# A selective-scan network on one core: one broadcast of B for two scans, and the skip term as a diagonal product

## The chip, the cores and the metric

The kernel runs on one core of one Trainium2 chip. The metric is the device time of one execution in microseconds (us). The core has a tensor engine (PE in the profile, with its weight loads as PEld), a vector engine (DVE), a scalar engine (ACT), GpSimd (POOL) and a sync engine (SP), which issues the transfers here. PE writes its products to PSUM[...]; the other tiles lie in SBUF.

## The reference

An input of 32 images (512 channels, 32x32 pixels) goes through four blocks in turn, with a group normalisation over 16 channels between them: channel weights from a discrete cosine transform (L0), a grouped 3x3 convolution (L1), a pyramid of selective scans (L2), and a channel attention that samples neighbouring channels (L3). The change lies in L2. Cut to what matters:

```python
def _ssm(x, xw, dtw, dtb, Al, Dv, g, be):       # x: [B, D=256, L], n = 16 states
    xd = einsum('bdl,kd->blk', x, xw)
    dts, Bs, Cs = split(xd)                      # 8, 16 and 16 columns
    delta = softplus(einsum('blr,dr->bld', dts, dtw) + dtb)
    dA  = exp(delta[..., None] * -exp(Al))       # per channel and state
    dBx = delta[..., None] * Bs[:, :, None, :] * xt[..., None]
    h = h * dA + dBx                             # a scan over L
    y = sum over n of h * C  +  xt * Dv          # Dv: the skip term
    return layernorm(y, g, be)
```

Each image has three resolutions: 1024 pixels (twice, forward and backward), 256 and 64 pixels (both directions). The scan is run for 256 channels and 16 states.

## The kernel before

**Tiles and units.** A scan tile has 128 partitions, which are 32 channels times 4 states, and 1024 columns. At full resolution (function `fine`) one direction of one image takes 2 halves `d` of the channels x 4 groups `k` of states x 4 groups `q` of channels = 32 such units; 64 calls of `fine` make 2048 units. The coarse resolutions (function `both`) pack several pieces in one tile and make 640 more scans, of which each pair shares one product tile.

One fine unit is this:

- PE multiplies `sb` (B, held in bfloat16 parts) with `sel_b[:, k, :]`, in two matmuls of 512 columns, into a PSUM tile `pb` (L1266). This puts the four states' rows of B onto the 128 partitions. It depends on `k` but not on `q`. The ring `pb` has two tiles of two banks each.
- ACT computes `da` = exp(delta * A) from the loaded tile `dt` (L1273); the ring `da` has two tiles.
- DVE multiplies `pb` in place with delta * x, which lies in the same `dt` (L1279).
- DVE scans over the 1024 columns with `da` and `pb` into `h` (L1212, the helper `scan`); six `h` tiles.
- POOL multiplies `h` with the loaded broadcast of C, `cb` (L1287).

After four units (`q` = 0 to 3) PE sums over the states by a product with `sel_y`, into two PSUM accumulators of one bank each, `y0` and `y1b`, one for each half of the columns (L1295). After the four `k` of one `d`, the scan input is loaded to `yv` (L1304), and DVE adds the skip term for each half in one instruction, yv = yv * Dv + accumulator (L1309). That frees the accumulators for the next `d`. A layer norm follows after both `d` (`layer_norm`, L1142 to L1165).

`both` treats its own skip term otherwise: the helper `skip_weights` (L1214) lets ACT write a diagonal matrix of Dv to the tile `dg`, a ring of one; PE adds its product with the input to the accumulator (L1476), and ACT copies the accumulator to SBUF (L1488).

**Order.** Nothing is issued in source order. Every operation is recorded with an engine, an estimated duration, what it reads and writes, and a key: a due time of 100 per image, with 84 scan units to an image. `Clock.key(ahead)` gives the key of the current unit less so many units. At the end `Plan.order` walks through a model of the engines: whenever an engine is free it takes the ready operation with the lowest key, if the ring buffers that it needs are free. Rings marked as ordered (`pb` is one) hand out their buffers in order of the buffers' keys, which is the key of the first operation that asks unless one is set. The outcome is a fixed order on each engine, and the engines then run in that order, waiting on each other. The constants on top (`B_AHEAD` for the broadcast, `A_AHEAD` for the exponential, `L_AHEAD` for loads, `DB_AHEAD` for the product) say how many units ahead of its scan an operation is due. `INPUTS` holds the keys, within 100 per image, between which the first convolution's products for `f1` are spread (function `scan_inputs`). Several images are in work at once: while one is scanned, the next ones' transforms, convolutions and projections fill PE, ACT and POOL.

Of the kernel before, what the change touches and what calls it, by code (L numbers as in the profile page):

```python
# [11 lines left out]
ALU = mybir.AluOpType  # L12
# [3 lines left out]
HW = 1024  # L16
IMG = 32
GC = 16
NS = 16
NQ = 4  # L20
# [4 lines left out]
HB = 512  # L25
# [3 lines left out]
UNITS = 84  # L29

FRONT = (30.9, 63.6)
INPUTS = (109.0, 112.0)
Z = (86.2, 90.1)
DOWN = 114.3
LOWER = (11.8, 36.0)
# [4 lines left out]
SPECTRA = (51.7, 128.4)  # L40
EVACUATE = 85.0
LN_LATE = 10.1
B_AHEAD, A_AHEAD, L_AHEAD, DB_AHEAD = 5.8, 5.9, 14.7, 1.3


class Buf:
# [175 lines left out]
def t_mm(n, count=1):  # L222
    return count * (0.06 + 1.02 * n / 512)


def t_dve(n):
    return 0.11 + n / 970
# [11 lines left out]
def kernel(ctx: ExitStack, tc: tile.TileContext, t: dict, out: bass.AP):  # L239
    nc = tc.nc  # L240
# [108 lines left out]
    xw, A, Dv, G, BE, dtb = [], [], [], [], [], []  # L349
# [46 lines left out]
    pl = Plan(rings)  # L396
# [16 lines left out]
    def pe(fn, dur, r, w, key, acq=()):  # L413
        return pl.op("PE", dur, fn, r, w, key, acq)

    def act(fn, n, r, w, key, ptr=False, acq=()):
        return pl.op("ACT", t_act(n, ptr), fn, r, w, key, acq)

    def dve(fn, n, r, w, key, acq=()):
        return pl.op("DVE", t_dve(n), fn, r, w, key, acq)  # L420
# [793 lines left out]
    def skip_weights(lv, d, key):  # L1214

        dg = pl.buf("dg")
        act(
            lambda: nc.scalar.activation(dg.t, ident, AF.Copy, scale=Dv[lv][:, d : d + 1]), P, [ready],
            [dg], key, True,
        )  # L1220
        return dg
# [10 lines left out]
    def fine(lv, f, pre, S, rev, ck):  # L1232


        sb, cd, dd = pre.pop(f"{lv}_{HW}")
        pl.cross = pl.BESIDE
        if rev:
            raised(S["y1"], S["y2"], ck.key())
        pl.cross = pl.CROSS
        yv = []  # L1240
        for d in range(2):
            acc = [pl.buf("y0"), pl.buf("y1b")]
            dt = []
            for q in range(4):
                ch = slice((d * 4 + q) * 32, (d * 4 + q + 1) * 32)
                z = pl.buf("dt")
                dt.append(z)
                spread(
                    lambda z=z: z.t, lambda i, ch=ch: dd.t[:, ch, :].rearrange("a c l -> c a l"),
                    P * HW * 8, [(dd, (d, h)) for h in range(2)], [z], ck.key(L_AHEAD - q),  # L1250
                )
            for k in range(NS // NQ):
                cb = pl.buf("cb")
                spread(
                    lambda cb=cb: cb.t,
                    lambda i, k=k: cd.t[k * NQ + i : k * NQ + i + 1].to_broadcast([32, HW]),
                    P * HW * 4, [cd], [cb], ck.key(5),
                )
                hs = []
                for q in range(4):  # L1260
                    g = d * 4 + q
                    pb, da, h = pl.buf("pb"), pl.buf("da"), pl.buf("h")

                    def bcast(pb=pb, k=k):
                        for cols in halves:
                            nc.tensor.matmul(  # L1266
                                pb.t[:, cols], lhsT=sel_b[:, k, :], rhs=sb.t[:, cols],
                                start=True, stop=True,
                            )

                    pe(bcast, 0.55, [sb], [pb], ck.key(B_AHEAD))
                    act(
                        lambda da=da, z=dt[q], k=k, g=g: nc.scalar.activation(  # L1273
                            da.t, z.t[:, 1, :], AF.Exp, scale=A[lv][:, k, g : g + 1]
                        ),
                        HW, [dt[q]], [da], ck.key(A_AHEAD), True,
                    )
                    dve(
                        lambda pb=pb, z=dt[q]: nc.vector.tensor_mul(pb.t, z.t[:, 0, :], pb.t), HW,  # L1279
                        [dt[q], pb], [pb], ck.key(DB_AHEAD),  # L1280
                    )
                    pl.op(
                        "DVE", 2.21, lambda h=h, da=da, pb=pb: scan(h.t, da.t, pb.t, rev), [da, pb], [h],
                        ck.key(),
                    )
                    pool(
                        lambda h=h, cb=cb: nc.gpsimd.tensor_mul(h.t, h.t, cb.t), HW, [h, cb], [h],  # L1287
                        ck.key(),
                    )
                    hs.append(h)  # L1290
                    ck.u += 1
                for i, cols in enumerate(halves):
                    def add(i=i, cols=cols, hs=hs, acc=acc, k=k):
                        for q in range(4):
                            nc.tensor.matmul(  # L1295
                                acc[i].t[q * 32 : (q + 1) * 32, :], lhsT=sel_y, rhs=hs[q].t[:, cols],
                                start=(k == 0), stop=(k == NS // NQ - 1),
                            )

                    pe(add, 1.3, hs, [acc[i]], ck.key(2))  # L1300
            y = pl.buf("yv")
            yv.append(y)
            dma(
                lambda y=y, d=d: nc.sync.dma_start(y.t, f.t[d]), P * HW * 4, [(f, d)],  # L1304
                [(y, 0), (y, 1)], ck.key(8),
            )
            for i, cols in enumerate(halves):
                dve(
                    lambda i=i, cols=cols, acc=acc, y=y, d=d: nc.vector.scalar_tensor_tensor(  # L1309
                        y.t[:, cols], in0=y.t[:, cols], scalar=Dv[lv][:, d : d + 1], in1=acc[i].t,  # L1310
                        op0=ALU.mult, op1=ALU.add,
                    ),
                    HB, [(y, i), acc[i]], [(y, i)], ck.key(3),
                )
        pl.cross = pl.BESIDE
        if not rev:
            S["y1"] = pl.buf("y1")
        y1 = S["y1"]
        for i, cols in enumerate(halves):
            yb = [(yv[d], i) for d in range(2)]  # L1320

            def yc(d, cols=cols):
                return yv[d].t[:, cols]

            def yo(d, cols=cols):
                return y1.t[:, d, cols]

            ob = [(y1, (d, i)) for d in range(2)]
            layer_norm(
                lv, yc, yb, yc if rev else yo, yb if rev else ob, HB, ck.key() + (0.0 if rev else LN_LATE)  # L1330
            )
            if not rev:
                continue
            g = pl.buf("g2")
            for d in range(2):
                dma(
                    lambda d=d, g=g, cols=cols: nc.sync.dma_start(g.t[:, d, :], S["zs"].t[d, :, cols]),
                    P * 2048, [(S["zs"], (d, i)), yb[d]], [(g, d)], ck.key(),
                )
                pool(  # L1340
                    lambda d=d, yo=yo, yc=yc: nc.gpsimd.tensor_add(yo(d), yo(d), yc(d)), HB,
                    [yb[d], ob[d]], [ob[d]], ck.key(),
                )
                pool(
                    lambda d=d, yo=yo, g=g: nc.gpsimd.tensor_mul(yo(d), yo(d), g.t[:, d, :]), HB,
                    [ob[d], (g, d)], [ob[d]], ck.key(),
                )

    def both(lv, f, pre, ysum, below, n, ck):


        sb, cd, dd = pre.pop(f"{lv}_{n}")
# [12 lines left out]
        acc = [pl.buf("y0"), pl.buf("y1b")]  # L1365
# [8 lines left out]
        for d in range(2):  # L1374
            dt = pl.buf("dt")
# [9 lines left out]
                )  # L1385
            for k0 in range(0, 4, nk):
                pb = pl.buf("pb")

                def bcast(pb=pb, k0=k0):
                    for h in range(2):  # L1390
                        if nk == 1:
                            src = sb.t.rearrange("p (o l) -> p o l", o=1).to_broadcast([96, 2, n])
                            nc.tensor.matmul(  # L1393
                                pb.t[:, halves[h]].rearrange("p (o l) -> p o l", o=2),
                                lhsT=sel_b[:, k0, :], rhs=src, start=True, stop=True,
                            )
                            continue
                        for k in range(h * nk // 2, (h + 1) * nk // 2):
                            src = sb.t.rearrange("p (o l) -> p o l", o=1).to_broadcast([96, 4, n])
                            nc.tensor.matmul(  # L1400
                                pieces(pb.t)[:, k, :, :], lhsT=sel_b[:, k0 + k, :], rhs=src,
                                start=True, stop=True,
                            )
# [21 lines left out]
                for r in range(2):  # L1425
                    da, h = pl.buf("da"), pl.buf("h")
# [46 lines left out]
            dg = skip_weights(lv, d, ck.key(8))  # L1473
# [7 lines left out]
        y = pl.buf("yv" if n > 64 else "yc")  # L1481
# [398 lines left out]
```

## Time and profile before

| | |
|---|---|
| median of three timed runs | 11386.0 us (11367.82 to 11386.98) |
| profiled execution, its own time | 11408.22 us |
| its span | 11406.1 us |
| granted PE clock, mean | 0.861 |
| busy: DVE / POOL / PE / ACT | 9938.1 / 9544.0 / 9375.9 / 8259.6 us |
| fine scans and coarse scans together (L1212) | 2688, 2275 ns each |
| broadcasts of B at full resolution (L1266) | 2048, of two matmuls each |
| skip-term instructions at full resolution (L1309) | 256 |

The durations in the sections below come from the one profiled execution. A row of a group gives line, engine, operation, output and inputs with shapes, count, then busy us in all and mean ns of one, then the idle time of the engine just before such instructions, and what ended most of it. A row of the waits reads: who waited, for whom, us in total, how often, the longest in us.

### The profile page before, as it was taken

To read this page: it belongs to the slowest core of one execution; us is meant where nothing else is said; L and a number is where in the kernel's file an instruction comes from. 1 tells how busy PE (TensorE), PEld (TensorE's weight loads), DVE (VectorE), ACT (ScalarE), POOL (GpSimd) and SP (SyncE) were. 2 spreads that over 40 slices of the span, in tenths; PEclk is the share of its full clock that TensorE was granted. 3 is DMA by queue.
4 is the path that set the end of the run, shared out by engine and by line. 5 is a ranking of instruction groups with operands and counts; after the bars stand their busy time and mean duration, and the time that the engine had idled before them with its cause. 6 is when DMAs were issued, how large, how long until landed. Compare 5 with 4: busy or idle time off the path is not lost. (4 is left out here: it accounts for less than half of the span.)

```text
span 11406.1 us, 152013 instructions
## 1 busy us (share of the span) xinstructions
PE 9375.9 (82%) x47512; PEld 4155.3 (36%) x47512; DVE 9938.1 (87%) x8861; ACT 8259.6 (72%) x15684; POOL 9544.0 (84%) x7759
## 2 busy tenths in 40 slices
PE   7888888888888888888888888888888888878765
PEld 4444433334333343333333343333433333332221
DVE  1875889998899989999899999899889998999997
ACT  4677777777778777777777777777777776667664
POOL 2775878898889888888888988898888898889885
PEclk7888889888889888898888988898898987888877
DMA  5665677776767777777767777777677766776654
GB/s 153 167 173 164 182 197 195 186 194 186 212 179 202 188 188 191 204 198 202 191 183 189 204 199 189 189 189 186 190 199 196 187 180 181 199 192 185 168 134 136
DMA packets 931019, 2116.80 MB, mean 186 GB/s; under 512 B 240033, under 2 KB 372537, under 8 KB 917785
## 3 DMA queue, kind: packets, MB, share of 16 engines
q1 hardware_dynamic: 930192, 2107.01, 69.5%
q8 instruction: 376, 6.16, 0.2%
q14 instruction: 433, 3.55, 0.1%
q10 hardware_dynamic: 18, 0.09, 0.0%
HBM read 1677.04 MB, written 429.52 MB: 185 GB/s over the span
## 5 line engine op out<-in xcount | busy, mean ns | idle before, releaser
L1212 DVE TENSOR_TENSOR_SCAN h_all<-da,pb 128x1024 f32<-128x1024 f32 x2688 | 6069.7, 2275 | 296.2 <-ACT da L1435 78.3
L1287 POOL TENSOR_TENSOR h_all<-h_all,cb 128x1024 f32<-128x1024 f32 x2048 | 4818.1, 2363 | 859.9 <-DVE h_all L1212 582.7
L1273 ACT ACTIVATE da<-dt,w_Al 128x1024 f32<-128x1024 f32 x2048 | 2337.1, 1145 | 1171.5 <-DVE h_all L1212 902.5
L1279 DVE TENSOR_TENSOR pb<-dt,pb 128x1024 f32<-128x1024 f32 x2048 | 2462.4, 1218 | 322.7 <-PE pb L1266 276.1
L1266 PE MATMUL pb<-sb,sel_b 96*128 96x512 bf16 x4096 | 1390.4, 426 | 888.0 <-DVE h_all L1212 797.2
L1455 POOL TENSOR_TENSOR h_all<-h_all,cb 128x1024 f32<-128x1024 f32 x640 | 1509.3, 2363 | 20.8 <-DVE h_all L1212 7.4
L1266 PEld LDWEIGHTS <-sel_b 96*128 96x128 bf16 x4096 | 402.4, 107 | 2032.8 <-issue 1998.0
L952 PE MATMUL mm<-x,wt 128*128 128x512 f32 x2048 | 1027.8, 626 | 54.8 <-ACT x L482 18.9
L899 PE MATMUL mm<-pk,wk 99*32 99x512 f32 (+1 forms) x6024 | 904.2, 688 | 113.8 <-DMA pk<-in_xp 19.9
L1444 ACT ACTIVATE da<-dt,w_Al 128x255 f32<-128x255 f32 x2048 | 899.4, 500 | 97.6 <-DVE h_all L1212 79.7
L1295 PE MATMUL y<-h_all,w_sel_y 128*32 128x512 f32 x4096 | 784.4, 724 | 33.5 <-POOL h_all L1287 27.2
L617 PE MATMUL mm<-w_dct,sx 128*128 128x128 f32 x3968 | 651.2, 319 | 94.6 <-ACT sg L460 24.7
L617 PEld LDWEIGHTS mm<-w_dct,sx 128*128 128x128 f32 x3968 | 583.6, 225 | 237.7 <-ACT sg L460 50.1
L1295 PE MATMUL y1b<-h_all,w_sel_y 128*32 128x512 f32 x4096 | 647.7, 663 | 0.0
L952 PE MATMUL mm<-y,w_out_w 128*128 128x512 f32 x1024 | 576.2, 655 | 0.1
L952 PEld LDWEIGHTS mm<-x,wt 128*128 128x128 f32 x2048 | 387.5, 198 | 492.5 <-issue 284.5
L1112 POOL TENSOR_TENSOR g<-g,g 128x512 f32<-128x512 f32 (+2 forms) x384 | 392.9, 1023 | 144.6 <-ACT g L1111 134.5
L1096 PE MATMUL mm<-xd,dtw 64*128 64x512 f32 (+2 forms) x768 | 417.4, 628 | 79.2 <-ACT xd L1066 11.7
L1142 PE MATMUL mm<-ln,ones_d 128*128 128x512 f32 (+1 forms) x768 | 433.1, 662 | 59.9 <-ACT ln L1154 30.7
L1407 DVE TENSOR_TENSOR pb<-dt,pb 128x1024 f32<-128x1024 f32 x320 | 387.7, 1218 | 108.5 <-PE pb L1393 86.6
L974 PE MATMUL mm<-f,wt 128*128 128x256 f32 (+1 forms) x1984 | 421.6, 357 | 21.7 <-ACT f L982 6.0
L1142 PE MATMUL mm<-yv,ones_d 128*128 128x512 f32 x640 | 380.6, 691 | 40.1 <-ACT mm L921 7.2
(292 smaller groups left out, 16188.4 us busy)
## 6 DMA issues: line engine op xcount, KB each, us to landing
dt<-dd SPq DMA_DIRECT2D x2048, 256.0 KB, 7.3
cb<-cd SPq DMA_DIRECT2D x2048, 128.0 KB, 4.8
pk<-in_xp SPq DMA_DIRECT2D x753, 297.0 KB, 5.5
dd<-g SPq DMA_DIRECT2D x256, 512.0 KB, 5.1
xr<-x SPq DMA_DIRECT2D x128, 512.0 KB, 6.3
yv<-fs SPq DMA_DIRECT2D x128, 512.0 KB, 5.1
dt<-ddm SPq DMA_DIRECT2D x512, 128.0 KB, 3.9
sx<-in_x SPq DMA_DIRECT2D x124, 512.0 KB, 4.7
```

The source lines that it names most:

```text
L617: nc.tensor.matmul(ps.t[:, j * P : (j + 1) * P], lhsT=sx.t[:, 1, i : i + P], rhs=dct, start=True, stop=True,)
L899: nc.tensor.matmul(ps.t[32 * q : 32 * q + 32, r0 * IMG : r1 * IMG].rearrange("p (r k) -> p r k", k=IMG), lhsT=wk.t[:, q, 32 * dy : 32 * dy ...
L952: nc.tensor.matmul(ps.t, lhsT=w(k)[:, m * P : (m + 1) * P], rhs=r()[:, cols], start=(k == 0 and not opened), stop=(k == len(rhs) - 1),)
L1142: lambda d=d: nc.tensor.matmul(ps.t[:, 0:n], lhsT=ones_d, rhs=of(d), start=(d == 0), stop=(d == 1)),
L1212: nc.vector.tensor_tensor_scan(v[0], v[1], v[2], 0.0, ALU.mult, ALU.add)
L1266: nc.tensor.matmul(pb.t[:, cols], lhsT=sel_b[:, k, :], rhs=sb.t[:, cols], start=True, stop=True,)
L1273: lambda da=da, z=dt[q], k=k, g=g: nc.scalar.activation(da.t, z.t[:, 1, :], AF.Exp, scale=A[lv][:, k, g : g + 1]),
L1279: lambda pb=pb, z=dt[q]: nc.vector.tensor_mul(pb.t, z.t[:, 0, :], pb.t), HW,
L1287: lambda h=h, cb=cb: nc.gpsimd.tensor_mul(h.t, h.t, cb.t), HW, [h, cb], [h],
L1295: nc.tensor.matmul(acc[i].t[q * 32 : (q + 1) * 32, :], lhsT=sel_y, rhs=hs[q].t[:, cols], start=(k == 0), stop=(k == NS // NQ - 1),)
L1444: lambda da=da, quads=quads, q=q, g=g, body=body, k0=k0: nc.scalar.activation(pieces(da.t)[:, 0, q, body], quads(1)[:, q, body], AF.Exp, s ...
L1455: lambda h=h, k0=k0: nc.gpsimd.tensor_mul(pieces(h.t), pieces(h.t), cbv()[:, k0 : k0 + nk, :].rearrange("p k (o l) -> p k o l", o=1).to_br ...
```

## The change

Three things are changed. At full resolution the broadcast of B is made once for two units that follow each other (`q` = 0, 1 and `q` = 2, 3): the first unit's product goes from the broadcast's tile `src` to a second `pb` tile, the second unit's product is made in place in `src`. The keys by which the two tiles are handed out are set by hand, and so is that of the coarse scans' tile. Second, the skip term at full resolution is made as `both` makes it: a diagonal matrix from ACT, a float32 product on PE that closes the accumulation, and a copy of the accumulator to `yv` on ACT, in place of the instruction on DVE. Third, three key constants move.

```diff
-INPUTS = (109.0, 112.0)
+INPUTS = (109.0, 123.2)
...
-B_AHEAD, A_AHEAD, L_AHEAD, DB_AHEAD = 5.8, 5.9, 14.7, 1.3
+B_AHEAD, A_AHEAD, L_AHEAD, DB_AHEAD = 8.0, 5.9, 14.7, 1.8
...
-                    pb, da, h = pl.buf("pb"), pl.buf("da"), pl.buf("h")
-
-                    def bcast(pb=pb, k=k):
+                    da, h = pl.buf("da"), pl.buf("h")
+
+
+                    if q % 2 == 0:
+                        src, pb = pl.buf("pb"), pl.buf("pb")
+                        src.key, pb.key = (ck.key(2.9), len(pl.ops)), (ck.key(1.0), len(pl.ops))
+                    else:
+                        pb = src
+
+                    def bcast(pb=src, k=k):
...
-                    pe(bcast, 0.55, [sb], [pb], ck.key(B_AHEAD))
+                    if q % 2 == 0:
+                        pe(bcast, 0.55, [sb], [src], ck.key(B_AHEAD))
...
                     dve(
-                        lambda pb=pb, z=dt[q]: nc.vector.tensor_mul(pb.t, z.t[:, 0, :], pb.t), HW,
-                        [dt[q], pb], [pb], ck.key(DB_AHEAD),
+                        lambda pb=pb, src=src, z=dt[q]: nc.vector.tensor_mul(pb.t, z.t[:, 0, :], src.t), HW,
+                        [dt[q], src], [pb], ck.key(DB_AHEAD),
                     )
...
-                                start=(k == 0), stop=(k == NS // NQ - 1),
+                                start=(k == 0), stop=False,
...
+            dg = skip_weights(lv, d, ck.key(8))
             for i, cols in enumerate(halves):
-                dve(
-                    lambda i=i, cols=cols, acc=acc, y=y, d=d: nc.vector.scalar_tensor_tensor(
-                        y.t[:, cols], in0=y.t[:, cols], scalar=Dv[lv][:, d : d + 1], in1=acc[i].t,
-                        op0=ALU.mult, op1=ALU.add,
+                pe(
+                    lambda i=i, cols=cols, acc=acc, y=y, dg=dg: nc.tensor.matmul(
+                        acc[i].t, lhsT=dg.t, rhs=y.t[:, cols], start=False, stop=True
                     ),
-                    HB, [(y, i), acc[i]], [(y, i)], ck.key(3),
+                    t_mm(HB), [(y, i), dg], [acc[i]], ck.key(3),
+                )
+                act(
+                    lambda i=i, cols=cols, acc=acc, y=y: nc.scalar.copy(y.t[:, cols], acc[i].t), HB,
+                    [acc[i]], [(y, i)], ck.key(3),
                 )
...
             for k0 in range(0, 4, nk):
                 pb = pl.buf("pb")
+                pb.key = (ck.key(2.9), len(pl.ops))
```

## The prediction

> **What bounds the kernel now.** I read the page first, then the busy time by stage, the DVE groups with shapes kept apart, the waits, and the instruction order of both programs, which is fixed when they are built. First the page: the span and part 1.
>
> ```profile
> span 11406.1 us, 152013 instructions
> PE 9375.9 (82%) x47512; PEld 4155.3 (36%) x47512; DVE 9938.1 (87%) x8861; ACT 8259.6 (72%) x15684; POOL 9544.0 (84%) x7759
> ```
>
> No engine is full: DVE leads, 1468 us idle, with POOL 394 us of work behind it. By stage (busy us of PE, PEld, DVE, ACT, POOL, then granted clock):
>
> ```profile
> 0.00:285.00 285.00, 202.47 (x988) 137.69 (x989) 56.16 (x117) 137.32 (x312) 78.74 (x115) 0.75 0.54 153
> 5000.00:7000.00 2000.00, 1672.62 (x8738) 741.95 (x8737) 1825.67 (x1630) 1508.16 (x2886) 1755.19 (x1427) 0.88 0.72 193
> 9000.00:10500.00 1500.00, 1232.82 (x5924) 492.15 (x5922) 1364.06 (x1085) 1047.94 (x1893) 1326.29 (x1046) 0.86 0.73 190
> ```
>
> In the steady part DVE is at 91%, POOL at 88%, PE at 84 to 82%. DVE sets the pace, through rows that wait now and then for a partner. About 456 of its 1468 idle us lie in the first 1000 us (1000 less 56.2, 239.2 and 248.3 busy), a filling phase with few scans, which the change hardly touches. The groups that carry the steady part:
>
> ```profile
> L1212 DVE TENSOR_TENSOR_SCAN h_all<-da,pb 128x1024 f32<-128x1024 f32 x2688 | 6069.7, 2275 | 296.2 <-ACT da L1435 78.3
> L1279 DVE TENSOR_TENSOR pb<-dt,pb 128x1024 f32<-128x1024 f32 x2048 | 2462.4, 1218 | 322.7 <-PE pb L1266 276.1
> L1266 PE MATMUL pb<-sb,sel_b 96*128 96x512 bf16 x4096 | 1390.4, 426 | 888.0 <-DVE h_all L1212 797.2
> L1309 DVE SCALAR_TENSOR_TENSOR yv<-yv,w_Dv,y1b 128x512 f32<-128x512 f32 x128 | 94.2, 736 | 22.3 <-PE y1b L1295 21.4
> L1309 DVE SCALAR_TENSOR_TENSOR yv<-yv,w_Dv,y 128x512 f32<-128x512 f32 x128 | 94.1, 735 | 75.8 <-PE y L1295 70.9 <-PE y1b L1295 4.8
> ```
>
> The change takes hold of L1279's wait for its broadcast, L1266's wait for a scan, and L1309 with its wait. From the waits:
>
> ```profile
> ACT da L1273 <- DVE h_all L1212: 902.5, 712, 6.5
> PE pb L1266 <- DVE h_all L1212: 797.2, 703, 5.6
> DVE pb L1279 <- PE pb L1266: 276.1, 246, 8.2
> DVE h_all L1212 <- ACT da L1273: 39.8, 47, 4.1
> ```
>
> TensorE stands 703 times at a broadcast until a scan frees one of the two pb buffers; 246 times the broadcast is then late for the product. ACT runs ahead of DVE: it waits 902.5 us for scans, and scans wait 39.8 us for it. Rows for what is added:
>
> ```profile
> L1488 ACT COPY yv<-y1b 128x512 f32<-128x512 f32 x32 | 18.7, 583 | 0.7 <-PE y1b L1476 0.7
> L1218 ACT ACTIVATE dg<-wide,w_Dv 128x128 f32<-128x128 f32 x128 | 50.7, 396 | 16.1 <-PE y1b L1476 15.7
> L1540 PE MATMUL mm<-t,wide 128*128 128x512 f32 x496 | 319.4, 730 | 53.1 <-ACT mm L1557 23.2 <-DMA t<-xr 15.7 <-ACT mm L921 3.5
> L1550 ACT ACTIVATE t<-mm,w_out_b 128x512 f32<-128x512 f32 x248 | 168.7, 680 | 192.1 <-PE mm L952 184.1 <-DMA dt<-ddc 5.2 <-DMA cb<-cdc 1.2
> ```
>
> [...] the trace has 1218. I expect no other price when the product goes to the other pb tile.
>
> **The change part by part.** Sums are against the profiled execution: 11,408.2 us, of which 11,406.1 are span. The median of the three timed runs, 11,386.0, lies 22 below; I subtract that at the end.
>
> *DVE work.* L1309 goes: 94.2 + 94.1 = -188.3 us. L1279 stays at 2048 products of 1218 ns, L1212 as it is.
>
> *Broadcast wait.* 2048 of 4096 broadcast matmuls go: 1390.4/2 = 695 us of busy PE (modelled ends). What matters is the cover: DVE work between the scan that frees a buffer and the product that needs the new broadcast in it. Joining the trace to the program's order, which names the buffer of every row, I get for before: 604 products with under 2.0 us of cover waited 161 us in all; 588 with 2.0 to 2.5 us waited 57 (0.096 each); 856 with more, 60 (0.070 each). Short covers arise because two products in a row each need a fresh broadcast, and the second one's buffer was freed only one product (1.2 us) earlier. In the changed order only the first product of a pair needs a broadcast; the second works in place on the same one. With the durations above, none of the 1024 has under 2.0 us of cover: 519 have 2.0 to 2.5 (one scan, 2.275), 505 more. At the same prices: 519 x 0.096 + 505 x 0.070 = 85 us, against 276: -191. Bounds: nothing gained, and all 276.
>
> *Wait before L1309.* 22.3 + 75.8 = 98.1 us go with it, but in half the cases a layer norm follows, whose products now come one engine later. I keep two thirds: -65 (bounds 0 and -98).
>
> *ACT and PE.* 256 copies at L1488's 583 ns are 149 us, 128 diagonals at 396 ns are 51: +200 us on an engine with 3146 us idle. The 256 float32 skip products cost what L1540's identity products do: 248 in 319.4 us, 1.29 us each, +330 on PE, so PE ends at 695 - 330 = 365 us less. Behind each copy on ACT stand exponentials that scans wait for; scans wait 78.3 + 39.8 + 38.9 = 157 us for ACT today. I add a quarter: +40. Lower bound zero; upper, every copy passes its duration and a wait like L1550's (192.1/248 = 0.77 us) to a scan: 256 x (0.583 + 0.77) = 346.
>
> *At no cost.* The skip product waits for the yv load on PE instead of DVE; no wait of L1309 was for a DMA, so the load is early (if it were late, broadcasts behind it on PE would be too). SP issues the same number of transfers. INPUTS spreads the 16 f1 products of an image over 14.2 instead of 3 key units; the exponentials counted in ACT's order between f1's first eviction and the coarse scans stay within a few units of before (47 and 48 in one image, 42 and 31 in another), so the coarse inputs aren't later. The other key edits only set the order that I counted. The tail gains one hop, some 2 us.
>
> *Sum.* -188 - 191 - 65 + 40 + 2 = -402 us. Part of it returns: a DVE that no longer waits for PE meets POOL, ACT and loads sooner, and POOL has 88% in the steady part. No row prices this; from nothing to all. I take a quarter, which leaves -300: 11,408 - 300 - 22 = **11,085 us**.
>
> **The rivals.** *Given back.* DVE's freed time turns into waiting for POOL, through the six h buffers, and for ACT. For: POOL's 9544.0 us against DVE's 9750 after the cut. Against: scans wait under 10 us for POOL's products today, and POOL waits 582.7 us for scans. Then only some 60 to 180 us remain: about 11,270.
>
> *PE relief carries further.* L1266 held PE 797 us; half the broadcasts might free half of that, and with it DVE's waits on other matmuls (L1407 86.6, layer norm 31.7, statistics some 106, h buffers held by y1b 45.6; 270 in all). With all the 402 kept and half of these: about 10,850.
>
> *Slower: ACT's queue.* Each copy sits on ACT behind a skip product, which sits on PE behind adds that wait for POOL; the exponentials behind the copy start late and the scan waits. It decides from 402/256 = 1.6 us of DVE time per copy, if nothing else is given back. L1550's 0.77 us of wait plus 0.58 is 1.35 before any slack in the two da buffers; at 2.2 us per copy the time would be 11,386 + 256 x 0.6 = 11,540. Against it: ACT's 902.5 us of running ahead, and L1488, the same copy, waits a few us in all.
>
> That the change does nothing would need a broadcast that isn't shared; the order shows 2048 broadcast matmuls instead of 4096.
>
> **How the numbers follow.** Likeliest case 57% (its own range 10,950 to 11,200); given back 14% (11,200 to 11,360); carried further 12% (10,750 to 10,950); ACT's queue 14% (above 11,410); no difference, within 0.2% or 23 us, about what a measurement here can tell, 3%. Faster 0.83, same 0.03, slower 0.14. From 10,840 to 11,380 leaves out the slower case and a few hundredths at the lower end.
>
> **What would show it.** Right: DVE busy near 9750; L1279 waiting for the broadcast for under 120 us; PE's wait for scans at the broadcast well below 797; no L1309; ACT near 8460; a span near 11,100. Given back: DVE busy down, but new waits of L1212 on POOL, ACT or h buffers as large as those removed. ACT's queue: L1212 waiting for L1273's successor for hundreds of us, and the copy's own idle time above 1 us each. Wrong altogether would be a product into the other pb tile that takes clearly more than 1218 ns: 0.1 us more on 1024 of them is 102 us.

## The result, and the profile after

The changed kernel takes 11,367.6 us (median of 20 runs, 11,344.8 to 11,379.0) against 11,384.7 us before (20 runs, 11,360.8 to 11,407.2): a ratio of 0.9982, 95% interval 0.9975 to 0.9988. That is 0.18% or some 20 us faster, of the 300 forecast. The profiled execution took 11,370.4 us. First its page: the span, part 1, and the groups that answer to those shown of before.

```profile
span 11368.1 us, 149323 instructions
PE 9192.7 (81%) x45976; PEld 4046.6 (36%) x45976; DVE 9799.9 (86%) x8605; ACT 8413.5 (74%) x16068; POOL 9538.3 (84%) x7759
...
L1212 DVE TENSOR_TENSOR_SCAN h_all<-da,pb 128x1024 f32<-128x1024 f32 x2688 | 6060.7, 2274 | 374.9 <-ACT da L1281 82.1
L1287 DVE TENSOR_TENSOR pb<-dt,pb 128x1024 f32<-128x1024 f32 x2048 | 2458.8, 1226 | 338.3 <-DMA dt<-dd 140.9
L1273 PE MATMUL pb<-sb,sel_b 96*128 96x512 bf16 x2048 | 695.3, 425 | 552.3 <-DVE h_all L1212 505.6
```

DVE did lose work: 9938.1 to 9799.9 us. The broadcasts are halved (4096 to 2048 matmuls, L1273 now). But DVE's idle time, span less busy, rose from 1468 to 1568 us. The stages, in the columns used before:

```profile
5000.00:7000.00 2000.00, 1651.73 (x8480) 734.26 (x8479) 1801.71 (x1591) 1534.21 (x2956) 1756.17 (x1440) 0.87 0.73 194
9000.00:10500.00 1500.00, 1195.22 (x5769) 463.66 (x5768) 1361.79 (x1049) 1085.47 (x1974) 1352.60 (x1057) 0.88 0.74 194
```

In the middle DVE is less busy than before (1801.7 of 2000 us against 1825.7), and POOL as busy as before. Nothing became full. The waits show where the time went (who, for whom, us in all, times, longest):

```profile
DVE pb L1287 <- DMA dt<-dd: 140.9, 90, 6.4
DVE pb L1287 <- PE pb L1273: 112.0, 92, 4.8
DVE h_all L1212 <- ACT da L1281: 82.1, 69, 4.1
DVE h_all L1212 <- PE y1b L1303: 79.2, 43, 9.4
DVE yv L1153 <- PE mm L1142: 58.3, 33, 10.6
```

and on PE and ACT:

```profile
PE pb L1273 <- DVE h_all L1212: 505.6, 355, 8.0
PE y L1303 <- POOL h_all L1295: 161.2, 138, 3.5
ACT yv L1324 <- PE y L1318: 116.8, 57, 11.5
```

The wait for the broadcast fell as forecast, from 276.1 to 112.0 us, and PE's stand at the broadcast from 797.2 to 505.6. In exchange DVE waits more for loads of dt, for exponentials (39.8 before), for h buffers that the sums still hold and for the layer norm's products. PE, freed at the broadcast, now stands at the sum over states, waiting for POOL's product. ACT stands 57 times at the new copy. The lines of before that answer to these:

```profile
DVE pb L1279 <- DMA dt<-dd: 39.4, 38, 3.1
DVE h_all L1212 <- PE y1b L1295: 45.6, 50, 3.4
DVE yv L1153 <- PE mm L1142: 31.7, 31, 3.1
PE y L1295 <- POOL h_all L1287: 27.2, 30, 3.2
```

A place in the timeline of the changed kernel shows how such a wait comes about (start, duration, engine, line; in brackets the idle time before it and its releaser):

```profile
5000.56 0.69 ACT L634 ACTIVATE sx<-mm,sg 128x512 f32<-128x512 f32 x1 [1.31 <-PE mm L617]
...
5001.31 1.23 DVE L1287 TENSOR_TENSOR pb<-dt,pb 128x1024 f32<-128x1024 f32 x1 [3.14 <-DMA dt<-dd]
...
5001.90 0.59 ACT L1324 COPY yv<-y1b 128x512 f32<-128x512 f32 x1
...
5002.37 0.42 ACT L1218 ACTIVATE dg<-wide,w_Dv 128x128 f32<-128x128 f32 x1
5002.67 1.15 ACT L1281 ACTIVATE da<-dt,w_Al 128x1024 f32<-128x1024 f32 x1
...
5003.91 2.29 DVE L1212 TENSOR_TENSOR_SCAN h_all<-da,pb 128x1024 f32<-128x1024 f32 x1 [1.37 <-ACT da L1281]
```

DVE's product first waits 3.14 us for its dt load. On ACT the exponential stands behind a statistics step that itself waited for PE, and behind the new copy and the new diagonal (0.59 and 0.42 us); so the scan waits another 1.37 us. DVE, ACT, PE and a load have a part in it.

### The profile page after: what moved, and what is told of

The parts are those of the page before. It is cut to its first block, busy times and chain, and to the rows that moved or that the text cites. A ratio compares the mean times of both kernels' runs of the same rounds, so it can differ in the third digit from the quotient of the medians.

```text
span 11368.1 us, 149323 instructions
## 1 busy us (share of the span) xinstructions
PE 9192.7 (81%) x45976; PEld 4046.6 (36%) x45976; DVE 9799.9 (86%) x8605; ACT 8413.5 (74%) x16068; POOL 9538.3 (84%) x7759
## 5 line engine op out<-in xcount | busy, mean ns | idle before, releaser
L1212 DVE TENSOR_TENSOR_SCAN h_all<-da,pb 128x1024 f32<-128x1024 f32 x2688 | 6060.7, 2274 | 374.9 <-ACT da L1281 82.1
L1281 ACT ACTIVATE da<-dt,w_Al 128x1024 f32<-128x1024 f32 x2048 | 2338.2, 1145 | 1093.3 <-DVE h_all L1212 858.4
L1287 DVE TENSOR_TENSOR pb<-dt,pb 128x1024 f32<-128x1024 f32 x2048 | 2458.8, 1226 | 338.3 <-DMA dt<-dd 140.9
L1273 PE MATMUL pb<-sb,sel_b 96*128 96x512 bf16 x2048 | 695.3, 425 | 552.3 <-DVE h_all L1212 505.6
L1303 PE MATMUL y<-h_all,w_sel_y 128*32 128x512 f32 x4096 | 942.8, 728 | 169.4 <-POOL h_all L1295 161.2
L1303 PE MATMUL y1b<-h_all,w_sel_y 128*32 128x512 f32 x4096 | 682.1, 652 | 0.3 <-ACT yv L1501 0.3
L1273 PEld LDWEIGHTS <-sel_b 96*128 96x128 bf16 x2048 | 192.4, 105 | 1188.5 <-issue 1176.7
```

The lines of the kernel that those rows point to most:

```text
L1212: nc.vector.tensor_tensor_scan(v[0], v[1], v[2], 0.0, ALU.mult, ALU.add)
L1273: nc.tensor.matmul(pb.t[:, cols], lhsT=sel_b[:, k, :], rhs=sb.t[:, cols], start=True, stop=True,)
L1281: lambda da=da, z=dt[q], k=k, g=g: nc.scalar.activation(da.t, z.t[:, 1, :], AF.Exp, scale=A[lv][:, k, g : g + 1]),
L1287: lambda pb=pb, src=src, z=dt[q]: nc.vector.tensor_mul(pb.t, z.t[:, 0, :], src.t), HW,
L1303: nc.tensor.matmul(acc[i].t[q * 32 : (q + 1) * 32, :], lhsT=sel_y, rhs=hs[q].t[:, cols], start=(k == 0), stop=False,)
```

## The experiments

**Parts alone.** Four runs: each part of the change without the others, and one cut of DVE work in an unchanged order.

Only the broadcast shared, with the new constants; skip term on DVE as before (the diagonal is gone too, and the last sum over states closes the accumulation again):

```diff
             for i, cols in enumerate(halves):
-                pe( ... acc[i].t, lhsT=dg.t, rhs=y.t[:, cols], start=False, stop=True ... )
-                act( ... nc.scalar.copy(y.t[:, cols], acc[i].t) ... )
+                dve( ... nc.vector.scalar_tensor_tensor(y.t[:, cols], in0=y.t[:, cols], ... in1=acc[i].t ... ) ... )
```

> The changed kernel with its skip term put back on DVE as it was before, all else (shared broadcast, key constants) as changed. Theory D (DVE sets the pace, and the two parts cancel: one wins, the other loses): 11,160 to 11,230 us, the predicted 191 us less a part. Theory N (no engine sets the pace alone; work taken from DVE or PE is worth only the share of the time in which it stands on the chain): within 40 us of the kernel before, 11,345 to 11,400.

Measured: 11,319.8 us, ratio to the kernel before 0.9927 (0.9910 to 0.9944). That lies between the two theories' ranges, in neither.

Only the skip term moved (the kernel before, with the diagonal and the pair of operations marked - in the diff above in place of its DVE instruction):

> The kernel before with only the skip term moved to PE and ACT; broadcasts and key constants as before. Theory D with cancelling parts: slower, 11,450 to 11,550, since copies on ACT hold up exponentials. Theory N: within 40 us of the kernel before, 11,345 to 11,420, though it takes 188 us from DVE.

Measured: 11,494.2 us, 1.0093 (1.0078 to 1.0108). Slower by 0.9%, though DVE has 158 us less to do: as theory D with cancelling parts said, and outside theory N's range.

Only the constants:

```diff
-INPUTS = (109.0, 112.0)
+INPUTS = (109.0, 123.2)
-B_AHEAD, A_AHEAD, L_AHEAD, DB_AHEAD = 5.8, 5.9, 14.7, 1.3
+B_AHEAD, A_AHEAD, L_AHEAD, DB_AHEAD = 8.0, 5.9, 14.7, 1.8
```

> The kernel before with only the three key constants of the change. The order on every engine is made anew. If the constants alone cost what the two parts win (a rival to both theories), 11,500 to 11,650. Theory N and theory D: 11,360 to 11,440.

Measured: 11,366.6 us, 0.9979 (0.9972 to 0.9987): as much as the whole change. Both theories had allowed it; that the constants cost what the parts win is out.

The skip term's DVE instruction cut to one column, in the order of before:

```diff
-                        y.t[:, cols], in0=y.t[:, cols], scalar=Dv[lv][:, d : d + 1], in1=acc[i].t,
+                        y.t[:, cols][:, 0:1], in0=y.t[:, cols][:, 0:1], scalar=Dv[lv][:, d : d + 1], in1=acc[i].t[:, 0:1],
```

> The kernel before with the skip term's 256 DVE instructions cut from 512 columns to one; the rest of the skip term and of the accumulator's copy is left out, nothing is added anywhere and the order is that of before. About 0.55 us less on DVE 256 times, 140 us. Theory D: 11,230 to 11,260, nearly all of it. Theory N: 10 to 50 us faster, 11,335 to 11,375.

Measured: 11,344.0 us, 0.9958 (0.9944 to 0.9972). DVE's busy time fell by 128.6 us (9938.1 to 9809.5), 0.50 for each of the 256 instructions, whose duration went from 736 to some 205 ns; the time fell by 0.42%, some 48 us, within theory N's range. Theory D, on which the prediction was built, fails: DVE work taken away, with nothing put elsewhere, pays 0.37 us for each us (0.25 to 0.50 by the interval).

**Which engine is worth what.** Two larger cuts in the order of before, about equal on two engines (b_dve also clears the h tiles once at the start, since the last columns are no longer written):

```diff
-    scan(h.t, da.t, pb.t, rev)
+    scan(h.t[:, 0:896], da.t[:, 0:896], pb.t[:, 0:896], rev)     # b_dve
...
-    nc.gpsimd.tensor_mul(h.t, h.t, cb.t)
+    nc.gpsimd.tensor_mul(h.t[:, 0:896], h.t[:, 0:896], cb.t[:, 0:896])   # b_pool
```

> The kernel before, same order, with the 2048 scans at full resolution cut from 1024 to 896 columns (the last columns are left out): about 0.27 us less each, 560 us less on DVE. Theory D (DVE sets the pace): 10,850 to 10,950. Theory N (DVE work is worth its share of the chain that ended last, 4 of the 14 to 15% of the span that the chain covers, near 0.28, as the narrowed skip term's 45 us for some 140 showed): 150 to 200 us faster, 11,190 to 11,240.

> The kernel before, same order, with POOL's 2048 products at full resolution cut from 1024 to 896 columns (the rest of C is left out): about 0.28 us less each, 565 us less on POOL. If POOL is the hidden bound: 10,900 to 11,050. Theory N, by POOL's 1 of 14 to 15% of that chain: 40 to 100 us faster, 11,290 to 11,350. Theory D: less than 30 us.

Measured: b_dve 11,180.6 us, 0.9822 (0.9809 to 0.9835); b_pool 11,369.5 us, 0.9978 (0.9970 to 0.9986). Part 1 of the page of b_dve, then of b_pool:

```profile
PE 9321.6 (83%) x47512; PEld 4107.5 (37%) x47512; DVE 9423.0 (84%) x8861; ACT 8236.0 (74%) x15684; POOL 9537.5 (85%) x7760
```

```profile
PE 9288.2 (82%) x47512; PEld 4122.7 (36%) x47512; DVE 9936.8 (87%) x8861; ACT 8258.7 (73%) x15684; POOL 9011.1 (79%) x7759
```

515 us less on DVE (0.25 for each of the 2048 scans) bring 1.78%, 203 us: 0.39 for each, as in the small cut. 533 us less on POOL (0.26 for each product) bring 0.22%, 25 us: 0.05 for each, though POOL is nearly as busy as DVE. (The granted clock was 0.867 in skip_narrow and 0.868 in b_dve, against 0.865 before. Within the runs of the kernel before, 0.001 of it goes with 5 to 7 us; by that estimate some 13 us of the one gain and 22 of the other may be the clock's, and the work itself worth 0.27 and 0.35.) This line stood on the page of before, and I hadn't used it: the chain of work that ended last, by engine.

```profile
DVE 4%; PE 3%; DMA 2%; issue 2%; ACT 2%; POOL 1%; SPq 0%; DVEq 0%; ACTq 0%; POOLq 0%
```

The chain could be followed back only over the last 15% of the span. Of the 14% that the line sums to, DVE has 4 (0.28) and POOL 1 (0.07): near the measured 0.37 to 0.39 and 0.05. In this kernel it says that no engine sets the pace, and whose work pays. But a sample of 15% of the span in whole per cent gives no second digit: from it theory N had 40 to 100 us for b_pool, and 25 came; for b_dve it had 150 to 200, and 203 came. Longer chains agree in kind (the page of skip_only follows 38% of the span: DVE 10, PE 7, POOL 3), while on the changed kernel's page the chain breaks off at once and every engine has 0%. PE has nearly DVE's share in these lines; no run cuts PE's work in the order of before.

**What the moved skip term costs.** Three causes for the 48 us between the changed kernel and the shared broadcast alone. Two cuts in the order of the changed kernel, one to the products and one to the copies:

```diff
-    nc.tensor.matmul(acc[i].t, lhsT=dg.t, rhs=y.t[:, cols], start=False, stop=True)
+    nc.tensor.matmul(acc[i].t[:, 0:1], lhsT=dg.t, rhs=y.t[:, cols][:, 0:1], start=False, stop=True)   # a_mmnarrow
...
-    nc.scalar.copy(y.t[:, cols], acc[i].t)
+    nc.scalar.copy(y.t[:, cols][:, 0:1], acc[i].t[:, 0:1])     # a_copynarrow
```

> The changed kernel with the skip products on PE cut from 512 columns to one, in the same order; the rest of the skip term is left out. Three causes are weighed for the 48 us that lie between the changed kernel (11,368) and the one that shares the broadcast alone (11,320). P (the products lengthen the time until the accumulators, and the h buffers behind them, are free, and load PE): 11,310 to 11,335. Q (copies stand at the head of ACT's queue until the product is done, with exponentials behind them): the wait stays, somewhat shorter, 11,340 to 11,360. T (200 us more of ACT work cost by themselves): unchanged, 11,360 to 11,375.

> The changed kernel with ACT's copies of the accumulators cut from 512 columns to one, in the same order; the layer norm then reads mostly the scan's input, the rest is left out. About 0.4 us less on ACT 256 times, 100 us. T: 11,310 to 11,335. Q and P: 11,350 to 11,370, since the copies wait for PE as before.

Measured: a_mmnarrow 11,385.0 us, 0.9993 (0.9984 to 1.0002), no faster than the changed kernel's 0.9982, and above the range of all three causes. Part 1 of its page:

```profile
PE 9095.4 (80%) x45976; PEld 4077.3 (36%) x45976; DVE 9802.2 (86%) x8605; ACT 8411.4 (74%) x16068; POOL 9539.2 (84%) x7759
```

This looks as if P failed, but it doesn't decide. The products' own groups fell by 190 us (138.8 + 135.9 to 44.5 + 40.7), PE's busy time by 97 only; the sums over states took longer, 734 and 664 ns, where the changed kernel has 728 and 652. The granted clock was 0.853 on the mean of 13 runs (at most 0.855), against 0.866 in the 20 of the changed kernel (at least 0.864). Within those 13 runs a clock higher by 0.001 goes with a time shorter by some 5 us, within the 20 by some 3 us. By these slopes the 0.012 between the two would be worth 35 to 60 us, an estimate. If they hold across the two, which no run shows, the shorter products won some 20 to 50 us, which is P's size, and lost them to the clock; P stays open.

a_copynarrow 11,350.1 us, 0.9967 (0.9955 to 0.9979), in the range of Q and P: 0.15% for 99 us of ACT work (0.39 for each copy), at the changed kernel's clock of 0.866, and the intervals touch. T fails as the cause of 48 us.

Then two for which the planner makes a new order: the copy on DVE, and the copy held back in the plan (`cross` is the delay after which the planner takes an operation to be ready).

```diff
-                act(
-                    lambda ...: nc.scalar.copy(y.t[:, cols], acc[i].t), HB,
+                dve(
+                    lambda ...: nc.vector.tensor_copy(y.t[:, cols], acc[i].t), HB,      # a_dvecopy
...
+                late_copy = act( ... nc.scalar.copy ... )
+                late_copy.cross = 3.0                                                   # a_late
```

> The changed kernel with the accumulators copied by DVE instead of ACT; the products on PE stay. DVE takes back about 150 us. Q and T: 11,310 to 11,345, ACT's queue is free again. P: 11,365 or more, and more yet if DVE's 150 us count.

> The changed kernel, where the planner is told that the copy on ACT can start only 3 us after its product, so that it puts more work ahead of it on ACT. No work is changed. Q: 11,325 to 11,350, the copy's wait for the product (116.8 us in the changed kernel) falls below 40. T and P: 11,360 to 11,380.

Measured: a_dvecopy 11,361.3 us, 0.9965 (0.9953 to 0.9977), between the two expectations. a_late 11,316.5 us, 0.9928 (0.9916 to 0.9941), some 9 us below Q's range, with the copy's wait gone from 116.8 to 10.5 us:

```profile
ACT yv L1324 <- PE y L1318: 10.5, 2, 9.1
```

That looked like the cause. The next two runs tested it: the same hold-back where the skip term alone is moved, and a control that makes a new order without aiming at anything.

```diff
-OUTPUT = (112.5, 123.5)
+OUTPUT = (113.5, 124.5)       # a_ctrl, on the changed kernel
```

> The kernel with the skip term alone moved (11,494), where the planner again takes the copy on ACT to be ready only 3 us after its product. Q (the copies' wait at the head of ACT's queue is what the moved skip term costs): the wait for the product falls from 97.7 to below 30 us and the time to 11,400 to 11,450. Rival R (the gain of the first such run was a chance of the new order): anywhere, 11,470 to 11,520 if nothing but the order's luck counts.

> A control: the changed kernel with the due times of an unrelated stage (the keys OUTPUT) moved by one key unit, which makes the order on every engine anew and aims at nothing. R: it moves by tens of us, as far as the 51 us that the late copy won. Q: within 25 us of 11,368, with the copy's wait for its product still above 80 us.

Measured: skip_late 11,461.7 us, 1.0060 (1.0046 to 1.0074): 0.33% better than its like, less than Q said, with the wait down from 97.7 to 12.9 us. a_ctrl 11,302.6 us, 0.9928 (0.9916 to 0.9941), with the copy's wait nearly as it was. The line of a_ctrl's waits:

```profile
ACT yv L1324 <- PE y L1318: 101.2, 56, 9.7
```

The control won as much as the hold-back. So a new order by itself moves the time by as much as the effects in question, and Q isn't shown: two gains of 0.54 and 0.33%, both the right way, but no larger than the control's 0.54.

**Several orders of each kernel.** So the two kernels were compared under the same perturbations of unrelated due times: OUTPUT one unit later or earlier, and the gate's keys Z one unit later (87.2, 91.1).

> The kernel before with the keys OUTPUT one unit later, the same control that won 65 us in the changed kernel; no work is changed. C (the order alone moves the time by tens of us, either way): anywhere from 11,330 to 11,460. I (the control's win belongs to the changed kernel): within 15 us of 11,390.

> The kernel before with the keys OUTPUT one unit earlier. C: anywhere from 11,330 to 11,460, at least 25 us from one of the other two orders of this kernel. I: within 15 us of 11,390.

> The changed kernel with the keys OUTPUT one unit earlier. C: 11,290 to 11,420. If the change is worth what the shared broadcast won (some 50 us) and the orders only scatter around it: 30 to 80 us below the kernel before under the same perturbation.

> The kernel before with the keys Z (the gate's products) one unit later. C: anywhere from 11,330 to 11,460. I: within 15 us of 11,390.

> The changed kernel with the keys Z one unit later, partner of the kernel before with the same. C: 11,290 to 11,420, and 30 to 80 us below its partner if the change is worth some 50 us on the mean.

> The kernel with the skip term alone moved (11,494), with the keys OUTPUT one unit later. If the moved skip term costs by itself: 60 us or more above the kernel before under the same perturbation, 11,430 to 11,530. If its 105 us were one order's bad luck: within 40 us of that kernel.

Ratios to the kernel before, with their intervals:

| order | kernel before | changed kernel | difference |
|---|---|---|---|
| as it is | 1 | 0.9982 (0.9975 to 0.9988) | -0.18% |
| OUTPUT + 1 | 0.9923 (0.9910 to 0.9936) | 0.9928 (a_ctrl) | +0.05% |
| OUTPUT - 1 | 0.9969 (0.9957 to 0.9981) | 0.9911 (0.9897 to 0.9924) | -0.58% |
| Z + 1 | 0.9941 (0.9927 to 0.9954) | 0.9976 (0.9967 to 0.9985) | +0.35% |
| mean | 0.9958 | 0.9949 | -0.09% |

Within a kernel the order alone scatters by 0.34 to 0.35% (standard deviation of four), 40 us. That is C, and more than C allowed: b_out1, b_z1 and a_outm1 fell below their ranges, by 25, 4 and 4 us. Theory I fails in all three orders of the kernel before. The forecast of 30 to 80 us for the change under the same perturbation came true in one pair (69 us) and not in the other (the changed kernel 37 us slower). The mean worth of the change over the four is -0.09% with a standard error of 0.20% (0.39%/2): nothing that these orders can tell. The 0.9927 of the shared broadcast alone, run in one order, lies within the orders of the kernel before (0.9923 to 1), so its gain isn't shown either, and nor is that of the constants (0.9979). All three other orders of the kernel before are faster than the one it came with. skip_out1, the skip term alone in another order: 11,431.5 us, 1.0037 (1.0025 to 1.0049), which is 1.14% of the time before above b_out1; with the first pair's 0.93% that is a cost in two orders, 1.0% on the mean of the pairs, or 0.7% against the mean of all four orders of the kernel before. It stands clear of the scatter: the three orders in which the skip term alone is moved (1.0037, 1.0060, 1.0093) lie above all four of the kernel before. The fastest order with all its work is the changed kernel with OUTPUT one unit earlier, 11,285.9 us. The granted clock alone doesn't explain the scatter: among the four orders of the kernel before the faster ones have the higher clock (0.864 to 0.873), but the changed kernel's four all lie between 0.8645 and 0.8661.

Averaging the same four profiles of each kernel (before, b_out1, b_outm1, b_z1; after, a_ctrl, a_outm1, a_z1) takes much of the luck out of the waits. Beside them stand the skip term alone moved (mean of skip_only and skip_out1) and the shared broadcast alone (share_only, one order):

| us | before, four orders | changed, four orders | skip term alone, two | broadcast alone, one |
|---|---|---|---|---|
| span | 11,347 | 11,328 | 11,468 | 11,326 |
| DVE busy | 9933 | 9795 | 9777 | 9956 |
| DVE idle | 1414 | 1533 | 1691 | 1370 |
| of it: products waiting for a broadcast, coarse ones too | 322 | 198 | 306 | 182 |
| skip term waiting for the sums (L1309) | 78 | none | none | 75 |
| scans waiting for ACT's da | 156 | 214 | 228 | 172 |
| products waiting for dt of `fine` | 51 | 129 | 95 | 90 |
| statistics waiting for POOL | 151 | 190 | 187 | 171 |
| layer norm's difference on yv waiting for PE | 30 | 59 | 63 | 33 |
| scans waiting for y1b's matmuls | 61 | 83 | 101 | 26 |

In the changed kernel two rows fall by 202 us together. Five rise by 225, and smaller ones by some 96 more; against them stand 137 us less DVE work. It isn't bad luck in one order: DVE is idle for 1492 to 1568 us in the four orders of the changed kernel, for 1356 to 1468 in those of the kernel before.

The two columns on the right show where the rises come from. With the skip term alone, the wait for broadcasts stays nearly as it was, and all five rows rise; DVE is idle 277 us longer for 156 us less work. With the broadcast alone, that for y1b falls, the layer norm's hardly rises, and those for da and POOL rise by 16 and 20 us only; the one for dt rises by 39. The five rows together rise by 225 us with the skip term alone and by 43 with the broadcast alone, in these few orders. So, but for dt, it is mainly the moved skip term that puts back what the shared broadcast took from DVE's waits. Four of these lines, from skip_only:

```profile
DVE h_all L1212 <- PE y1b L1295: 108.3, 77, 8.5
DVE h_all L1212 <- ACT da L1273: 94.3, 65, 4.6
DVE pb L1279 <- DMA dt<-dd: 82.2, 56, 5.8
DVE yv L1153 <- PE mm L1142: 53.1, 30, 10.0
```

## Why the prediction was wrong

*DVE work, -188.* Mis-sized: measured -138 (mean of four orders -137). The groups' own sums of DVE fall by 197 us, 10,432 to 10,235, but successive DVE instructions overlap in the records, 494 us of it before and 435 after. Summed over the groups, their own busy time was 5% and 4% above the engine's.

*Broadcast wait, -191.* Right in mechanism and nearly in size: 276.1 to 112.0, -164. The changed program's covers, joined to its trace, are what was counted: none under 2.0 us. The 549 products with 2.0 to 2.5 us of cover waited 111 us for PE, 0.20 each, twice the price taken from before; the 475 with more waited 24 us, 0.05 each. (Of these 135 us, 23 ended at other matmuls than the broadcast's.)

*Wait before L1309, -65.* 98.1 us went; the layer norm's difference took 27 back (31.7 to 58.3): -71.

*ACT, +40.* Scans wait 42 us more for L1281 (39.8 to 82.1), about 41 over all three kinds of exponential (157 to 198). As a count of exponentials it was right. As a statement of what moving the skip term costs it was far too low: the skip term alone, moved, costs 0.7 to 1.0%, while its 158 us of DVE work at 0.37 to 0.39 should have brought some 60 us. The bill is thus some 140 to 180 us, an estimate. The copies' duration accounts for little of it (a_copynarrow); the products' part is open (a_mmnarrow); the copies' wait at the head of ACT's queue may be some of it (skip_late, without that wait, is 0.33% faster than its like), and isn't shown. This is the rival "ACT's queue" only in part: exponentials add 72 us where DVE's idle time grows by 277, and the signs set down for it didn't come (L1212 waits 94.3 us for L1273 in skip_only, not hundreds; a copy's own idle time is 97.7/256 = 0.4 us, not above 1).

*PE, 365 us less.* PE's busy time fell by 183 only (9375.9 to 9192.7). The broadcasts took 695 off and the skip products added 275. The sums over states now cover 943 + 682 us, where they covered 784 + 648, with nearly the same mean each (728 and 652 ns; 724 and 663 before): they stand less close together. PE time wasn't in the sum.

*The tail, +2.* From the end of the last sum over states to the end of yv's second half it is 0.8 us before (11330.0 to 11330.8) and 3.2 after (11285.3 to 11288.5): +2.4.

*Covered at no cost.* The constants alone gave 0.9979. But waits for dt rose from 39.4 to 140.9 us. I had counted transfers, and the yv load, and no row for dt being needed earlier or loaded later. Both parts bring it (82.2 with the skip term alone, 90.0 with the broadcast alone), the constants little (50.3). Whether dt is needed earlier or loaded later wasn't tried.

*The step that failed.* Two did. The larger is the price of the moved skip term. Its three terms, -188 for DVE's work, -65 for the wait before L1309 and +40 for ACT, made -213 us; moved alone it cost 0.93 and 1.14% in two orders, +106 and +130 us. The prediction let the move lengthen the waits for exponentials and, within the -65, the layer norm's. With nothing else changed, the runs show waits for h buffers, dt loads and statistics longer as well, by 40, 44 and 36 us, beside 72 for exponentials and 33 for the layer norm. Which of product, copy and diagonal starts them stays open.

The second is the last step of the sum: "a DVE that no longer waits for PE meets POOL, ACT and loads sooner ... I take a quarter". It rested on "DVE sets the pace", read from busy shares of 91 and 88%. The fixed-order cuts put the worth of DVE work at 0.37 to 0.39 where the sum had 0.75; at that price the forecast's own 402 us would have left 150. That a wait removed pays no better than work removed is argued and not shown by a cut. What there is for it is the broadcast alone: waits for broadcasts 140 us below the mean of before, DVE's idle time 44 below, in one order. Together, over nine tenths came back: the first three terms, as measured, sum to some -400 us (138 + 164 + 98), while the span of the profiled execution fell by 38 and the median by 17.

The rival "given back", at 14%, comes nearest in kind; it was too mild in size (11,270, and no more than 11,360) and only partly right in its place. It named POOL, the h buffers and ACT. Waits for h buffers and exponentials did come, but cutting POOL's product brings 0.05 us for each, and dt loads, statistics and layer norm weren't named. Nor did its sign come: L1212's waits rose by 79 us (296.2 to 374.9), far less than those removed. "PE relief carries further" found no support: of the 292 us that PE no longer stands at the broadcast, 134 went into waiting for POOL's products at the sum. The signs set down for "right" came one by one (DVE's busy time down, the broadcast wait under 120, ACT near 8460), all but the span: they tell that the change did its work, and not what the work is worth.

*What I left out* is the order. Where an edit made the planner set a new order, the order alone was worth some 40 us (standard deviation of four); a forecast to 0.2% for one order was more than the profile can carry, and my chance of 3% for no difference, within 0.2%, which is where the result lies, left no room for it.

## What to carry to other kernels

Here four engines were busy at 72 to 87% and none was full, and busy time didn't price an edit: a microsecond cut from DVE brought 0.37 to 0.39, one cut from POOL 0.05, at 87 and 84% busy. In such a case cut some work from an engine in an unchanged order and measure what a microsecond of it brings, and compare the granted clock before reading the answer. The shares of the chain that ended last, 0.28 and 0.07 for the two, were a first hint, from 15% of the span. Moving work between engines can cost more than the work was worth: the skip term, made on PE and ACT, took 158 us off DVE and cost 0.7 to 1.0% of the time. Where a planner remakes the whole order after each edit, compare several orders of both versions before believing a difference of half a per cent, or a cause found in a single run.

## What the runs showed of the hardware

DVE instructions that follow each other overlap in the records, by 494 us in all before and 435 after: the 256 skip instructions, 736 ns each in their group, took 0.54 us each off the busy time in the changed kernel, and 0.62 where they alone were moved (158 us). The product of `pb` and `dt` into the other `pb` tile took about what it takes in place: L1287 has 1226 ns on the mean, 1230 for the first of each pair, which goes to another tile, and 1221 for the second, in place, against 1218 before.

The granted clock differed between these kernels. It was 0.865 before (27 runs), 0.858 with the broadcasts halved (share_only, 6 runs), 0.866 with the skip products added to that (20 runs), 0.853 with these cut to one column (a_mmnarrow, 13 runs), and 0.875 with the skip products added to the kernel before (skip_only, 5 runs). In each of these steps it was lower with less matmul work; but the whole change took PE's busy time from 9375.9 to 9192.7 us and left the clock where it was, 0.865 and 0.866. Only the step to a_mmnarrow keeps the order, and an order alone moved the clock from 0.864 to 0.873 in the kernel before. What sets the clock isn't shown.
